# Folded heads loaded ahead of the first attention, and two pairs of them per routing wait, in a two-layer block of attention and feed-forward

## The chip, the cores and the metric

One core of a Trainium2 chip. Times are device microseconds of one launch. The kernel before took 667.93 us, the median of three runs (667.68 to 668.8).

## What is computed

800 tokens (8 batches of 100) of width 512 pass four residual steps, each on a layer norm of the stream: a causal cross attention, a mixture of 8 experts of which each token takes 2, a latent cross attention with 16 heads, and a feed-forward with quantised weights and activations. Cut to what the change touches:

```python
x = x + _L0_xattn_ref(_layernorm(x), ctx_512, Wq, Wkv_expand, Wout)
x = x + _L0_ffn_ref(_layernorm(x), Wg, W1, W2, W3)
x = x + _L1_xattn_ref(_layernorm(x), ctx_512, Wq, w_kc_q, w_kc_kv, W_qr, W_kr, Wo)
x = x + _L1_ffn_ref(_layernorm(x), w_gate_up, w_down)

# in _L0_ffn_ref: each token's two best experts
scores = jnp.einsum('btd,ed->bte', x, Wg)
topk_s, topk_i = jax.lax.top_k(scores, TOP_K)

# in _L1_xattn_ref: three products in a row make the scored query
q_hk = (hidden_q @ Wq.T).reshape(b, s, H, K)
q_big = jnp.einsum('bshk,hkq->bshq', q_hk, w_kc_q)
q_r = jnp.einsum('bshq,hqr->bhsr', q_big, W_qr)
```

The three matrices of the last lines don't depend on the tokens. The kernel multiplies them into one matrix of 512 x 64 per head (the folded heads), in 8 pairs of heads.

## The kernel before

**Tiling.** Tokens lie in seven tiles of 128 rows, the last of 32. All matmuls of the steps that matter here are f32. TensorE (PE), VectorE (DVE) and ScalarE (ACT) run in the order in which the code is written (`tc.manual_schedule`, leaving at the spill branch and entered again behind it). GpSimd (POOL) and the SP queue, which issues most transfers, are ordered by the framework, by priority and by when a buffer comes free; each then works through its queue in that order.

**Stages.** First attention (to about 105 us), with the output projection of the last tiles mixed in; routing; a branch for tokens that no expert has room for; eight experts; second attention; quantised feed-forward. The change lies in the second to fourth, and in what is loaded ahead of the first.

**Folding a pair.** `fold_load(i)` (L698) loads one pair's three matrices in five transfers, some 1.1 MB, into `wq_p`, `kq_p` and `qr_p` of the pool `fw` (three buffers each, opened at L493 when the first attention's inputs are done with). `fold_first` (L722) is twelve recorded matmuls of 64 columns (L711) and a copy by ACT (`a_p`, L719); `fold_second` (L746) four matmuls of 512 columns (L749) and a copy by ACT (`f_p`, L753); `fold_third` four transposes (L759) and a copy by ACT into `wqf` (L760). `fold_beside` and `fold_turn` are another form of the first step for use between an expert's matmuls (L731, L741).

**Routing** (L765 to L835). The tokens of tiles 0 to 4 are scored and ranked first (`gate_scores`, `rank_choices`, `give_slots`), then tiles 5 and 6, whose projection was put last. Each ranking is a row of small DVE steps, with PE needed for the counts (L658, L661) and ACT for one exponential (L631). Then POOL scatters each tile's rows to the slots of their experts (`x_slot`, L686, 13 scatters). There are two stretches in which PE waits for DVE: in each, one pair is folded. Pairs 0 to 2 are loaded during the last batches of the first attention; each further load waits for a buffer.

**Branch.** `spilt` says whether a token found no slot. SP and the engines read it and jump over the block if not, which is so with these inputs. Tiles of the pool `sp` belong to that block.

**After the branch.** SP fetches the slots of experts 0 and 1 (`xg`, L1015), then three row blocks of the quantised feed-forward's weights (`gu`, L850), one of the down projection (`dn`, L855) and one pair. PE folds pairs 2 and 3 meanwhile, then transposes expert 0's slots (`columns_of`, L1040, copied into `xgT` by ACT and DVE, L1044 and L1042), and the experts begin.

**Experts** (L1101 on). Per expert: `gate_and_up` three times (L1109), the down product (L1175), and the next expert's transposes. Between them experts 0 to 3 fold pairs 4 to 7, one each, and load the next. DVE also quantises two blocks of `gu` per expert and, for experts 0 to 3, one of `dn`. Weights of expert e+2 are loaded into `ew` while e runs. Behind the last experts, `wq_p` and `qr_p` serve for output weights of the second attention (`load_wo`, `value_weights`). The rows come back from `x_acc`, and the rotary tables and contexts are loaded into pools that take the place of `ew` and `fw`.

Of the kernel before, what the change touches and what calls it, by code (L numbers as in the profile page):

```python
# [12 lines left out]
F32 = mybir.dt.float32  # L13
# [6 lines left out]
P = 128  # L20
B, S, D = 8, 100, 512
N = B * S
L, DC = 361, 128
KC = D // P
# [15 lines left out]
NH1, R1, CQ = 16, 64, 384  # L40
# [10 lines left out]
def tile_kernel(  # L51
# [7 lines left out]
    nc = tc.nc  # L59

    def open_pool(name, bufs=1, side="left"):
        guard = tc.tile_pool(name=name, bufs=bufs, side=side)
        pool = guard.__enter__()
        return pool, lambda: guard.__exit__(None, None, None)
# [90 lines left out]


    fold, close_fold = open_pool("fold", side="right")
    ate, close_ate = open_pool("attn0_early", side="right")
    at, close_at = open_pool("attn0")
    atw, close_atw = open_pool("attn0w", bufs=2)  # L160
# [28 lines left out]
    for t in range(4, NT):  # L189
# [7 lines left out]
        x_acc[NR:, :].rearrange("(n p) d -> p n d", p=P),  # L197
        zeros.unsqueeze(1).to_broadcast([P, SPARE // P, D]),
    )

    mask = at.tile([S, 4, S], BF16, tag="mask", name="mask")
    nc.gpsimd.memset(mask, 0.0)
# [277 lines left out]
    ew, close_ew = open_pool("ew", bufs=2, side="right")  # L480
# [9 lines left out]

    fw, close_fw = open_pool("fold_in", bufs=3, side="right")  # L493
    wqf = fold.tile([P, KC, NH1 * R1], F32, tag="wqf", name="wqf")

    gp, close_gp = open_pool("gate", side="right")
# [198 lines left out]

    def fold_load(i):  # L698
        wq_p = fw.tile([P, 2, D], F32, tag="wq_p", name=f"wq_p{i}")
        nc.sync.dma_start(wq_p, wq1[ds(2 * i * P, 2 * P), :].rearrange("(j p) d -> p j d", p=P))  # L700
        kq_p = fw.tile([P, 2, CQ // P, P], F32, tag="kq_p", name=f"kq_p{i}")
        qr_p = fw.tile([P, 2, CQ // P, R1], F32, tag="qr_p", name=f"qr_p{i}")
        for j in range(2):
            nc.sync.dma_start(kq_p[:, j], wkcq[2 * i + j].rearrange("(c p) k -> p c k", p=P))
            nc.sync.dma_start(qr_p[:, j], wqr[2 * i + j].rearrange("(c p) r -> p c r", p=P))
        return i, wq_p, kq_p, qr_p

    def fold_head(i, wq_p, kq_p, qr_p, j, pa=None):
        pa = bank() if pa is None else pa
        for c in range(CQ // P):  # L710
# [11 lines left out]
    def fold_first(*loads):  # L722
        pa = fold_head(*loads, 0)
        return fold_copy(*loads, fold_head(*loads, 1, pa))
# [21 lines left out]
    def fold_second(i, wq_p, a_p):  # L746
        pb = bank()
        for j in range(2):
            nc.tensor.matmul(  # L749
                pb[ds(R1 * j, R1), :], a_p[:, ts(j, R1)], wq_p[:, j, :], start=True, stop=True  # L750
            )
        f_p = fw.tile([P, D], F32, tag="f_p", name=f"f_p{i}", bufs=2)
        nc.scalar.copy(f_p, pb)  # L753
        return i, f_p

    def fold_third(i, f_p):
        pt = bank()
        for c in range(KC):
            nc.tensor.transpose(pt[:, ts(c, P)], f_p[:, ts(c, P)], ident)  # L759
        nc.scalar.copy(wqf[:, :, ts(i, P)], pt.rearrange("p (c r) -> p c r", c=KC))  # L760

    pairs_left = list(range(3, NH1 // 2))
    loaded = [fold_load(i) for i in range(3)]


    begin(6)
    po = bank()
    project_part(2, po, oT, wout_sb, KC, 0, 2)
# [34 lines left out]
    project_part(5, po, oT, wout_sb, KC, 0, KC)  # L803
    rank_choices(0, 5)
    give_slots(0, 5)
    part = fold_first(*loaded.pop(0))
    project_add(5, po)
    token_stats(mvs, 5, 6)
    token_scales(mvs, sd_all, rstd_all, 5, 7)
    nc.scalar.activation(sd0[:, 0:1], ln_eps, AF.Exp)  # L810
    for t in range(5, 7):
        gate_norm(t)
    part = fold_second(*part)
    loaded.append(fold_load(pairs_left.pop(0)))
    xT = gate_columns(5, 7)
    fold_third(*part)
    gate_scores(5, 7, xT)

    part = fold_first(*loaded.pop(0))
    rank_choices(5, 7)  # L820
    give_slots(5, 7)

# [6 lines left out]
    nc.vector.tensor_reduce(most, pn[:, :NE], AX.X, ALU.max)  # L829
    spilt = gp.tile([P, 1], I32, tag="spilt", name="spilt")  # L830
    nc.vector.tensor_scalar(spilt, most, float(CAP), None, ALU.is_gt)
    part = fold_second(*part)
    fold_third(*part)
    close_atw()
    close_at()  # L835

# [9 lines left out]
    def load_gate_up(n, pool=None):  # L846
        w = rows.tile([P, D], F32, tag="xn", name=f"gu{n}") if pool else qin.tile(
            [P, D], F32, tag="gu", name=f"gu{n}", bufs=GB
        )
        nc.sync.dma_start(w, wgu[ts(n, P), :])  # L850
        return n, w

    def load_down(n):
        w = qin.tile([P, NI], F32, tag="dn", name=f"dn{n}", bufs=1)
        nc.sync.dma_start(w, wdn[ts(n, P), :])  # L855
        return n, w
# [27 lines left out]
    gate_up_left = list(range(OT - LATER))  # L884
    HC = len(SLOTS)
    GB = 3
    gate_up_in = []

    def quantise_next():
        if gate_up_in:  # L890
            turn_gate_up(*quantise_gate_up(*gate_up_in.pop(0)))
            if gate_up_left:
                gate_up_in.append(load_gate_up(gate_up_left.pop(0)))

    in_order.__exit__(None, None, None)

    def slot_tiles(e):
# [15 lines left out]
    with tc.If(spills > 0, preferred_fallthrough_block=True):  # L913
# [38 lines left out]
        with tc.For_i(0, NE, 1, hint_engines=()):  # L952
            nc.gpsimd.iota(at_x, pattern=[[0, 1]], base=0, channel_multiplier=1)
            w12_e = sp.tile([P, KC, 2 * HE], F32, tag="spw", name="spw")
            for c in range(KC):
                gathered(w12_e[:, c, :], w12.rearrange("e d h -> (e d) h"), at_w[:, c : c + 1])
            w3_e = sp.tile([P, 3, D], F32, tag="sp3", name="sp3")
            for m, (m0, mr) in enumerate(HCH):
                gathered(
                    w3_e[:mr, m, :], w3.rearrange("e h d -> (e h) d"),  # L960
                    at_w[:mr, KC + m : KC + m + 1],
                )
            nc.vector.tensor_scalar(at_w[:, :KC], at_w[:, :KC], D, None, ALU.add)
            nc.vector.tensor_scalar(at_w[:, KC:], at_w[:, KC:], HE, None, ALU.add)
            with tc.For_i(0, NT, 1, hint_engines=()):
                x_t = sp.tile([P, D], F32, tag="spx", name="spx")
                gathered(x_t, x_all_rows, at_x)
                g_t = sp.tile([P, 1], F32, tag="spg", name="spg")
                gathered(g_t, spilt_gates, at_g)
                pt = bank()  # L970
                for c in range(KC):
                    nc.tensor.transpose(pt[:, ts(c, P)], x_t[:, ts(c, P)], ident)
                xT = sp.tile([P, KC, P], F32, tag="spxT", name="spxT")
                nc.scalar.copy(xT, pt.rearrange("p (c q) -> p c q", c=KC))
                hT = sp.tile([P, 3, P], F32, tag="sph", name="sph")
                for m, (m0, mr) in enumerate(HCH):
                    pw = bank()
                    ups = [(0, UP[m], mr)] if m < 2 else [(0, UP64, 64), (64, HE, 32)]
                    for j, cols in enumerate(([(0, m0, mr)], ups)):
                        for to, at_col, n in cols:  # L980
                            for c in range(KC):
                                nc.tensor.matmul(
                                    pw[ds(to, n), ds(j * P, P)], w12_e[:, c, ds(at_col, n)],
                                    xT[:, c, :], start=(c == 0), stop=(c == KC - 1),
                                )
                    s = sp.tile([P, P], F32, tag="sps", name="sps")
                    nc.scalar.activation(s[:mr], pw[:mr, :P], AF.Silu)
                    nc.vector.tensor_tensor(hT[:mr, m, :], s[:mr], pw[:mr, ds(P, P)], ALU.mult)
                py = bank()
                for m, (m0, mr) in enumerate(HCH):  # L990
                    nc.tensor.matmul(
                        py[:, :D], hT[:mr, m, :], w3_e[:mr, m, :], start=(m == 0), stop=(m == 2)
                    )
                y_t = sp.tile([P, D], F32, tag="spy", name="spy")
                nc.vector.tensor_scalar(y_t, py[:, :D], g_t, None, ALU.mult)
                nc.gpsimd.indirect_dma_start(
                    out=x_acc, out_offset=bass.IndirectOffsetOnAxis(ap=at_x, axis=0),
                    in_=y_t, in_offset=None, compute_op=ALU.add,
                )
                nc.vector.tensor_scalar(at_x, at_x, P, None, ALU.add)  # L1000
                nc.vector.tensor_scalar(at_g, at_g, P, None, ALU.add)
# [75 lines left out]

    behind_slots = tc.issue_after(slots[1][-1][1])
    behind_slots.__enter__()
    gate_up_in = [load_gate_up(gate_up_left.pop(0)) for _ in range(GB)]  # L1080
    down_in = load_down(0)
    while len(loaded) < 3:
        loaded.append(fold_load(pairs_left.pop(0)))


# [4 lines left out]
    in_order.__enter__()  # L1090

    nc.scalar.activation(most, ln_eps, AF.Silu)
    part = fold_first(*loaded.pop(0))
    following = fold_first(*loaded.pop(0))
    part = fold_second(*part)
    following = fold_second(*following)
    fold_third(*part)
    fold_third(*following)
    turned = columns_of(0, slots[0])
    gates = choices(0, slots[0])  # L1100

    for e in range(NE):
# [35 lines left out]
        part = None  # L1138
        gate_and_up(0)
        if loaded:  # L1140
            part = fold_beside(*loaded.pop(0))
            if pairs_left:
                loaded.append(fold_load(pairs_left.pop(0)))
        quantise_next()
        gate_and_up(1)
        if part:
# [77 lines left out]
    value_weights(6)  # L1224
    normed.append(layernorm(1))
    value_weights(7)
    close_fw()
    close_ew()

# [606 lines left out]
```

## Time and profile before

| what | us |
| --- | --- |
| median of three runs | 667.93 |
| the profiled execution's own time | 667.63 |
| its span, first to last instruction | 665.9 |
| PE matmul busy | 637.0 (96%) |
| DVE busy | 416.8 (63%) |
| ACT busy | 243.5 (37%) |
| POOL busy | 177.7 (27%) |
| mean granted PE clock | 0.979 |

The page cuts the span into 40 slices of 16.6 us; a digit is the busy share in tenths, PEclk the granted clock in tenths of full speed. A table by stage gives, for each stretch, its length and the busy time (and number) of instructions of each engine, then granted clock, share of the DMA engines, and GB/s. A line of the timeline has the start, the time, engine, line, operation, what is written from what, and in brackets how long the engine had been idle and what ended it. A matmul's end is modelled, its start is recorded. The chain of waits follows the work that ended last backwards; here it can be followed to 134 us and not further back, so the routing is read from the timeline.

### The profile page before, as it was taken

What the parts mean: (1) busy time and instruction counts of PE and PEld (TensorE: products, weight loads), DVE (VectorE), ACT (ScalarE), POOL (GpSimd) and SP (SyncE); (2) the same over time, 40 slices, a digit from 0 to 9 for tenths busy, and PEclk for the clock granted to TensorE, in tenths of its full rate; (3) what the DMA queues carried; (4) which work ended last, traced back from release to release, by engine and by line L of the source; (5) the groups of instructions that cost most, each with busy time, mean ns of one, the idle gap of its engine ahead of it and who ended that gap; (6) DMA issues with size and microseconds to landing.
All of it is one profiled execution on the core that took longest, in us unless ns stands there. A gap on an engine that the chain in (4) does not pass through costs nothing.

```text
span 665.9 us, 9840 instructions
## 1 busy us (share of the span) xinstructions
PE 637.0 (96%) x3471; PEld 411.5 (62%) x3471; DVE 416.8 (63%) x1058; ACT 243.5 (37%) x558; POOL 177.7 (27%) x191
## 2 busy tenths in 40 slices
PE   8999998689999999999999999999999999999995
PEld 5767755366677677558866766766666544444443
DVE  4865688407666553253148877877676456666687
ACT  3653454332212111231145655655555313222140
POOL 2232330600111122228604233234233002221021
PEclk9999999569999999999999999999999999999998
DMA  9800293789999998754300210210000301011211
GB/s 302 250 18 17 67 331 122 242 258 287 313 303 307 267 338 213 157 163 122 110 1 11 65 45 17 59 36 11 1 13 0 118 13 29 10 31 30 50 31 70
DMA packets 80289, 80.34 MB, mean 121 GB/s; under 512 B 41267, under 2 KB 54119, under 8 KB 80111
## 3 DMA queue, kind: packets, MB, share of 16 engines
q1 hardware_dynamic: 76543, 70.97, 36.4%
q0 software_dynamic: 3696, 8.72, 5.8%
q8 instruction: 28, 0.46, 0.3%
q14 instruction: 22, 0.18, 0.1%
HBM read 56.36 MB, written 16.50 MB: 109 GB/s over the span
## 4 chain that ended last, share of the span: by engine, by line
PE 66%; DVE 5%; DMA 4%; POOL 1%; ACT 1%; issue 1%; SPq 1%; POOLq 0%; ACTq 0%; DVEq 0%
PE bank L359 12%; PE bank L1109 11%; PE bank L1407 10%; PE bank L1382 8%; PE bank L1325 7%; PE bank L1175 6%; PE bank L1399 4%; PE bank L1566 3%; PE bank L1363 2%; PE bank L1040 1%; DMA qr_p<-in_wqr 1%; POOL e L1393 1%; DVE nm L1386 1%; DMA x_acc<-y,place 1%; DMA gu<-in_wgu 1%
## 5 line engine op out<-in xcount | busy, mean ns | idle before, releaser
L1393 POOL TENSOR_SCALAR e<-e,rs 128x361 f32<-128x361 f32 x51 | 61.4, 1205 | 126.2 <-DVE rs L1392 84.6
L359 PE MATMUL bank<-wvo,ctxT 128*128 128x512 f32 x192 | 83.9, 593 | 0.0
L1382 PE MATMUL bank<-kvT,qe 128*128 128x361 f32 (+1 forms) x208 | 78.6, 475 | 1.7 <-issue 1.0
L1109 PE MATMUL bank<-xgT,w 128*128 128x240 f32 (+1 forms) x384 | 75.5, 369 | 0.9 <-ACT xgT L1044 0.9
L1407 PE MATMUL bank<-pT,kvr 121*128 121x400 f32 x192 | 70.6, 503 | 1.4 <-ACT pT L82 0.8
L1109 PEld LDWEIGHTS bank<-xgT,w 128*128 128x128 f32 (+1 forms) x384 | 64.1, 181 | 12.4 <-issue 6.6
L1390 ACT ACTIVATE e<-bank,nm 128x361 f32<-128x361 f32 x100 | 56.5, 565 | 30.9 <-DVE nm L1386 21.9
L1386 DVE TENSOR_REDUCE nm<-bank 128x1 f32<-128x361 f32 x100 | 52.7, 528 | 17.3 <-PE bank L1382 16.6
L1399 PEld LDWEIGHTS bank<-ident,e 128*121 128x121 f32 x300 | 46.6, 184 | 26.9 <-POOL e L1393 3.9
L359 PEld LDWEIGHTS bank<-wvo,ctxT 128*128 128x128 f32 x192 | 36.2, 190 | 43.1 <-issue 42.6
L1186 POOL DMA_INDIRECT x_acc<-y,place x16 | 24.5, 1531 | 122.1 <-ACT y L1185 118.8
L1583 POOL TENSOR_TENSOR hid<-g,u 128x512 f32<-128x512 f32 (+1 forms) x17 | 20.5, 1215 | 114.2 <-ACT g L1574 74.8
L1399 PE MATMUL bank<-ident,e 128*121 128x128 f32 x300 | 49.6, 275 | 1.0 <-POOL e L1393 1.0
L1407 PEld LDWEIGHTS bank<-pT,kvr 121*128 121x128 f32 x192 | 33.9, 190 | 20.9 <-ACT pT L82 1.0
L1325 PE MATMUL bank<-xT,wqf 128*128 128x256 f32 (+1 forms) x192 | 43.8, 389 | 0.7 <-ACT xT L1310 0.7
L1175 PE MATMUL bank<-w,hT 128*128 128x512 f32 (+3 forms) x96 | 43.0, 595 | 0.3 <-DVE hT L1133 0.3
L324 POOL TENSOR_TENSOR s<-s,rs 100x800 f32<-100x800 f32 x16 | 24.4, 1523 | 70.7 <-DVE rs L323 30.5
L1325 PEld LDWEIGHTS bank<-xT,wqf 128*128 128x128 f32 x192 | 36.2, 190 | 7.4 <-ACT xT L1310 0.9
L1382 PEld LDWEIGHTS bank<-kvT,qe 128*128 128x128 f32 (+1 forms) x208 | 32.0, 186 | 11.7 <-issue 1.8
L82 ACT COPY pT<-bank 121x384 f32<-121x384 f32 (+3 forms) x55 | 24.4, 443 | 25.5 <-PE bank L1399 24.8
L80 DVE COPY ctxT<-bank 128x400 f32<-128x400 f32 (+2 forms) x23 | 13.2, 572 | 31.8 <-PE bank L1325 26.0
L1121 DVE TENSOR_TENSOR hT<-silu,bank 128x240 f32<-128x240 f32 x16 | 6.5, 404 | 38.0 <-ACT silu L1120 38.0
(260 smaller groups left out, 1022.2 us busy)
## 6 DMA issues: line engine op xcount, KB each, us to landing
w<-in_w SPq DMA_DIRECT2D x8, 1408.0 KB
gu<-in_wgu SPq DMA_DIRECT2D x22, 256.0 KB
w<-in_w SPq DMA_DIRECT2D x16, 256.0 KB
wq_p<-in_wq SPq DMA_DIRECT2D x8, 512.0 KB
wo<-in_wo SPq DMA_DIRECT2D x8, 512.0 KB
x_slot<-zeros SPq DMA_DIRECT2D x1, 3840.0 KB
kq_p<-in_wkcq SPq DMA_DIRECT2D x16, 192.0 KB
dn<-in_wdn SPq DMA_DIRECT2D x4, 704.0 KB
```

Of the source, the lines that this page charges most:

```text
L82: nc.scalar.copy(dst, src)
L359: nc.tensor.matmul(po[:, :D], lhs[:, c, ds(t * P, r)], rhs[:, c, :], start=(c == 0), stop=(c == chunks - 1),)
L1109: nc.tensor.matmul(po, w12_e[:, c, cols], xgT[:, c, :], start=(c == c0), stop=(c == c1 - 1))
L1175: nc.tensor.matmul(py[i][:n], hT[:mr, m, ds(s0, n)], w3_e[:mr, m, :], start=(m == 0), stop=(m == 2))
L1186: d = nc.gpsimd.indirect_dma_start(out=x_acc, out_offset=bass.IndirectOffsetOnAxis(ap=place[:, 0:1], axis=0), in_=y, in_offset=None, compu ...
L1325: nc.tensor.matmul(pq[:, i, :], wqf[:, c, ts(p0 + i, P)], xT[:, c, :], start=(c == 0), stop=(c == KC - 1),)
L1382: nc.tensor.matmul(ps[ds(to, n), :L], qe[:, ds(k0, n)], kvT, start=True, stop=True)
L1386: d = nc.vector.tensor_reduce(nm[:r], ps[:r, :L], AX.X, ALU.max, negate=True)
L1390: nc.scalar.activation(e[:r], ps[:r, :L], AF.Exp, bias=nm[:r], accum_out=sm[:r])
L1393: (nc.vector if odd else nc.gpsimd).tensor_scalar_mul(e[:r], e[:r], rs[:r])
L1399: nc.tensor.transpose(pt[:LP, c, :r], e[:r, ds(c * (LP - 1), LP)], ident[:r, :r])
L1407: nc.tensor.matmul(pc[:, :VC], kvr[:, c, :], pT[:, c, :], start=(c == 0), stop=(c == LC - 1))
```

## The change

1. The pool `fw` is opened ahead of the first attention's pools, with four buffers instead of three, and `fold_load` with it. Pairs 0 to 3 are loaded behind the first attention's inputs. Since `fw` now lies under the first attention's pool, the routing's tiles (`gp`) take part of the place of that pool.
2. In both routing waits two pairs are folded instead of one. After the first, two pairs are loaded instead of one.
3. The first three `gu` blocks and the first `dn` block are loaded ahead of the branch instead of behind the slot fetches. The pairs still left are then all loaded behind the slot fetches, and none in the experts.
4. So six pairs are folded ahead of the experts, and two beside experts 0 and 1.
5. The spill block uses the row tiles `xs` in place of five tiles of its own, and `ew` is closed before `fw`.

```diff
     fold, close_fold = open_pool("fold", side="right")
+    fw, close_fw = open_pool("fold_in", bufs=4, side="right")
     ate, close_ate = open_pool("attn0_early", side="right")
...
+    def fold_load(i):
...
+    pairs_left = list(range(4, NH1 // 2))
+    loaded = [fold_load(i) for i in range(4)]
...
-    fw, close_fw = open_pool("fold_in", bufs=3, side="right")
...
-    pairs_left = list(range(3, NH1 // 2))
-    loaded = [fold_load(i) for i in range(3)]
...
     give_slots(0, 5)
-    part = fold_first(*loaded.pop(0))
+    parts = [fold_first(*loaded.pop(0)) for _ in range(2)]
     project_add(5, po)
     token_stats(mvs, 5, 6)
     token_scales(mvs, sd_all, rstd_all, 5, 7)
     nc.scalar.activation(sd0[:, 0:1], ln_eps, AF.Exp)
     for t in range(5, 7):
         gate_norm(t)
-    part = fold_second(*part)
-    loaded.append(fold_load(pairs_left.pop(0)))
+    parts = [fold_second(*a) for a in parts]
+    for _ in range(2):
+        loaded.append(fold_load(pairs_left.pop(0)))
     xT = gate_columns(5, 7)
-    fold_third(*part)
+    for a in parts:
+        fold_third(*a)
     gate_scores(5, 7, xT)
 
-    part = fold_first(*loaded.pop(0))
+    parts = [fold_first(*loaded.pop(0)) for _ in range(2)]
     rank_choices(5, 7)
     give_slots(5, 7)
...
-    part = fold_second(*part)
-    fold_third(*part)
+    parts = [fold_second(*a) for a in parts]
+    for a in parts:
+        fold_third(*a)
     close_atw()
     close_at()
...
-    gate_up_in = []
...
+    gate_up_in = [load_gate_up(gate_up_left.pop(0)) for _ in range(GB)]
+    down_in = load_down(0)
     in_order.__exit__(None, None, None)
...
-                x_t = sp.tile([P, D], F32, tag="spx", name="spx")
+                x_t = xs[1]
...
     behind_slots = tc.issue_after(slots[1][-1][1])
     behind_slots.__enter__()
-    gate_up_in = [load_gate_up(gate_up_left.pop(0)) for _ in range(GB)]
-    down_in = load_down(0)
-    while len(loaded) < 3:
+    while pairs_left:
         loaded.append(fold_load(pairs_left.pop(0)))
...
         gate_and_up(0)
         if loaded:
             part = fold_beside(*loaded.pop(0))
-            if pairs_left:
-                loaded.append(fold_load(pairs_left.pop(0)))
...
     value_weights(7)
+    close_ew()
     close_fw()
-    close_ew()
```

More of the change, by code (lines that the diff above doesn't have):

```diff
@@ L199, in tile_kernel @@
     )
+    def fold_load(i):
+        wq_p = fw.tile([P, 2, D], F32, tag="wq_p", name=f"wq_p{i}")
+        nc.sync.dma_start(wq_p, wq1[ds(2 * i * P, 2 * P), :].rearrange("(j p) d -> p j d", p=P))
+        kq_p = fw.tile([P, 2, CQ // P, P], F32, tag="kq_p", name=f"kq_p{i}")
+        qr_p = fw.tile([P, 2, CQ // P, R1], F32, tag="qr_p", name=f"qr_p{i}")
+        for j in range(2):
+            nc.sync.dma_start(kq_p[:, j], wkcq[2 * i + j].rearrange("(c p) k -> p c k", p=P))
+            nc.sync.dma_start(qr_p[:, j], wqr[2 * i + j].rearrange("(c p) r -> p c r", p=P))
+        return i, wq_p, kq_p, qr_p
+    pairs_left = list(range(4, NH1 // 2))
+    loaded = [fold_load(i) for i in range(4)]
     mask = at.tile([S, 4, S], BF16, tag="mask", name="mask")
@@ L694, in give_slots @@
                 tc.add_to_no_dep_group("to_slots", d.ins)
[L698 to L706, printed above, removed]
     def fold_head(i, wq_p, kq_p, qr_p, j, pa=None):
@@ L972, in tile_kernel @@
                     nc.tensor.transpose(pt[:, ts(c, P)], x_t[:, ts(c, P)], ident)
-                xT = sp.tile([P, KC, P], F32, tag="spxT", name="spxT")
+                xT = xs[2].rearrange("p (c q) -> p c q", c=KC)
                 nc.scalar.copy(xT, pt.rearrange("p (c q) -> p c q", c=KC))
-                hT = sp.tile([P, 3, P], F32, tag="sph", name="sph")
+                hT = xs[3][:, : 3 * P].rearrange("p (m q) -> p m q", m=3)
                 for m, (m0, mr) in enumerate(HCH):
@@ L985, in tile_kernel @@
                                 )
-                    s = sp.tile([P, P], F32, tag="sps", name="sps")
+                    s = xs[4][:, :P]
                     nc.scalar.activation(s[:mr], pw[:mr, :P], AF.Silu)
@@ L993, in tile_kernel @@
                     )
-                y_t = sp.tile([P, D], F32, tag="spy", name="spy")
+                y_t = xs[5]
                 nc.vector.tensor_scalar(y_t, py[:, :D], g_t, None, ALU.mult)
@@ L1092, in tile_kernel @@
     nc.scalar.activation(most, ln_eps, AF.Silu)
[L1093 to L1098, printed above, removed]
+    parts = [fold_first(*loaded.pop(0)) for _ in range(2)]
+    parts = [fold_second(*a) for a in parts]
+    for a in parts:
+        fold_third(*a)
     turned = columns_of(0, slots[0])
```

## The prediction

> **What bounds the kernel now.** I read the slices first, then busy time by stage, then the timeline around the two routing waits, and last the chain of waits. The slices:
>
> ```profile
> span 665.9 us, 9840 instructions
> ...
> PE   8999998689999999999999999999999999999995
> ...
> PEclk9999999569999999999999999999999999999998
> DMA  9800293789999998754300210210000301011211
> ```
>
> TensorE is the bound nearly everywhere, except in slices 7 and 8 (116 to 150 us), where it has gaps and its clock is halved: the routing. By stage (span; busy us of PE, PEld, DVE, ACT, POOL; granted clock; DMA share; GB/s):
>
> ```profile
> 115.20:118.90 3.70, 1.12 (x5) 0.24 (x5) 3.10 (x12) 2.70 (x4) 2.56 (x3) 1.00 0.64 174
> 118.90:123.00 4.10, 3.57 (x24) 2.35 (x24) 0.64 (x2) 2.47 (x6) 3.19 (x4) 0.59 1.05 313
> 123.00:128.60 5.60, 3.37 (x23) 3.04 (x21) 2.63 (x18) 0.00 (x0) 4.27 (x5) 0.50 0.85 327
> 128.60:134.40 5.80, 3.09 (x8) 1.01 (x9) 3.06 (x18) 2.59 (x5) 2.26 (x3) 0.50 0.24 96
> 134.40:139.70 5.30, 5.27 (x24) 5.19 (x24) 0.00 (x0) 0.71 (x3) 0.58 (x1) 0.50 0.44 109
> ...
> 183.00:200.60 17.60, 17.60 (x91) 12.34 (x89) 11.84 (x29) 3.97 (x10) 3.06 (x2) 1.00 1.13 309
> ...
> 233.50:248.70 15.20, 15.20 (x70) 11.00 (x69) 8.14 (x24) 2.38 (x5) 3.05 (x2) 1.00 1.08 334
> ```
>
> An expert with a folded pair beside it takes 17.6 us, one without 15.2, PE full in both: a pair costs 2.4 us there. In the routing PE has 2 to 3 us free in each wait. The timeline there:
>
> ```profile
> 113.65 1.52 PE L711 MATMUL bank<-qr_p,kq_p 128*128 128x64 f32 x12
> ...
> 115.49 1.28 ACT L240 ACT_TABLE_LOAD   x1
> ...
> 118.86 1.09 PE L578 MATMUL bank<-ident,x_all 128*128 128x128 f32 x8 [2.26 <-DVE x_all L560]
> ...
> 128.62 0.27 ACT L719 COPY a_p<-bank 128x128 f32<-128x128 f32 x1 [6.39 <-remote]
> ...
> 144.63 0.98 PE L1040 MATMUL bank<-ident,xg 128*128 128x128 f32 x8
> ```
>
> The same L711 block takes 1.52 us at full clock and 2.82 (from 123.02) at half. The copy at 128.62 comes 2.78 us after the modelled end of its multiplications (125.84) and no row says why. L1040, which starts the experts, waits for the half-clock fold work in front of it (134.43 to 144.5). The chain of waits:
>
> ```profile
> 134.08 3.58 DMA x_slot<-x_all,to
> ...
> 144.41 6.66 DMA qr_p<-in_wqr
> 151.12 0.87 PE bank L731 x10
> ```
>
> The last scatter lands at 137.66, the slots are then fetched, and expert 0 stalls once more for a pair loaded late.
>
> **The change by parts.** Of eight pairs, four are folded ahead of the experts now (one per wait, two after the branch), four beside experts 0 to 3. After: six ahead (two, two, two) and two beside experts 0 and 1.
>
> *Experts 2 and 3.* Each loses 2.4 us of PE work. DVE becomes near-critical: after its product at 191.45 it runs without a break to the copy of xgT (L1042) at 199.71; PE from the end of the second gate_and_up (190.58) needs 2.59 + 0.97 + 5.15 = 8.71 without the fold, to 199.3. PE so waits 0.45 us for DVE: 1.95 each, **3.9** in sum (bounds 0, if the transfers bound this stage, and 4.8). Transfers: two pairs of 1.1 MB fewer there, and experts 4 to 6 run at 15.2 with shares of 0.9 to 1.2.
>
> *Expert 0.* It takes 18.85 us against 17.61 of expert 1. Its pair will be queued behind four slot fetches alone, not behind gu, dn and another pair as well: five issues of 0.45 us after 140, landed by about 145, needed at 147.5. **1.2** (bound 0).
>
> *First wait.* fold_first twice ends at 113.65 + 3.04 = 116.7, its second a_p copy at 117.0. The sqrt table load, which stands behind that copy on ACT, moves from 115.49 to 117.0, the sqrt ends at 118.6 instead of 118.03: x_all and the transposes come 0.57 late. PE has 0.86 us of fold_second more, so its gap shrinks from 2.26 to 0.9. ACT then has two f_p copies instead of one ahead of gT (0.47 more) and two wqf copies ahead of parts: parts end at 122.7 instead of 122.2, **0.5 late**. PE's second fold_third (0.55) lies inside that.
>
> *Clock.* It fell at 119.67 and rose at 143.57 by the trace's clock records. In the 3.4 us before the fall PE streamed for 13% (column counts over clock), and every stretch with 28% or more kept the clock. After, the same stretch holds eight L749 matmuls and is at 50%, the next at some 40%: I take full clock.
>
> *Second wait.* At full clock L601 takes half, L711 starts at 123.2, and 24 of it take 3.04: to 126.25, 0.4 after 125.84. Queued behind them on PE: the slot counts (L658, L661); on ACT the exponential that DVE waits for. The unexplained 2.78 us is bounded by 0 (the blocks at 113.65 and 134.43 had none) and 2.78 (same place, same instruction). I keep it whole, as that row is the nearest. So counts, scatter and branch come **0.4 late**.
>
> *Transfers in the routing.* More than before: one pair (1.1 MB) and gu and dn moved ahead of the branch (3 x 256 + 704 KB), 2.6 MB, 8 us at 320 GB/s. Room, by the shares above, from 115.2 to 134.4: 0.36 x 3.7 + 0.15 x 5.6 + 0.76 x 5.8 = 6.6 us. Up to 1.4 us runs over into the last scatter's landing; I take half, **0.7**.
>
> *After the branch.* PE starts at 134.85; 24 of L711 3.04, eight of L749 1.72, the rest 1.3: done at 141, where it took 10.1 us to 144.5. The second slot tile landed at 141.6 by the semaphore records; now 141.6 + 0.4 + 0.7 = 142.7, which becomes what L1040 waits for. 144.52 - 142.7 = **1.8** earlier.
>
> *Costed at nothing.* Four pairs ahead of attention: 4.4 MB, some 15 us, behind all its inputs on SP's queue, in 27 to 50 us where the DMA share is 0.03 to 0.08 and SP idles until 46; twenty issues of 0.47 us. Were that cover gone, x_acc rows would be late, which nobody reads before the first expert adds. POOL's 27 memsets and iotas for the routing (2.2 us at 2.5 to 4.8) now lie in memory that xn0 frees only during attention: POOL ends a share at 80.11 that PE takes at 81.94, so 1.8 is covered, 0.4 at most not. The second pair of loads in the first wait is five more issues on SP (2.3 us from 118); behind them are the x_acc rows of tiles 5 and 6, which no wait in the routing reads. The gu and dn loads, four issues of 0.4 us moved past the slot fetches, wait in SP's queue until L601 frees their place (123); behind them is the read of the spill flag at 132.85, so nine microseconds cover them, and a longer wait would delay the branch by its excess. The gate weights' load goes behind the four pairs and is wanted at 106. At the end the rotary tables can wait for the last value_weights (292.6) instead of 287.99; POOL would finish at 332 instead of 329 and PE takes the first rows at 339.8. Code in the spill branch isn't run.
>
> **Sum.** 1.8 + 1.2 + 3.9 = 6.9 us from the profiled execution's 667.63 (665.9 of span and 1.7 around it): 660.7. The median shown is 667.93, 0.3 more: **661.0**.
>
> **Rivals.**
> *No pause.* The 2.78 us aren't there again: scatter 2.4 early, the second slot tile at 139.9, PE ready at 138.5: 4.6 instead of 1.8, **658.2**. For it: two of three L711 blocks without pause; against: the same place.
> *The clock falls all the same*, at about 122, since PE then does little but transposes with waits between. L711 runs 124.9 to 130.2, the scatter is 1.6 late, and PE, at half clock with two pairs more ahead of the branch, reaches L1040 at 147.4: 2.9 late, less 5.1 of the experts: **665.7**. Against: a stretch at 28% kept the clock at 99 us. [...]
> *The slow block (slower).* If 123.02 to 128.6 was a rate, 465 ns per L711 multiplication under the transfers of that moment, and not a pause, and the clock is at half, 24 of them take 11.2 us from 124.9: the counts come at 136.1, 7.5 late, PE has fold work until 143.5, the branch's block runs 10.7 more, L1040 starts at 154.2, 9.7 late. Less 5.1: **672.5**. It decides as soon as L1040 comes after 149.6. For it: traffic in that wait grows; against: L711 at 134.43 went at 223 ns.
> *It does nothing*: transfers bound the experts (share 1.1), so that less PE work there is idle time, and the routing is 1 us slower for the ACT copies: **667.5**. Against: experts 4 to 6.
>
> **Numbers.** Forecast 0.43, no pause 0.24, clock falls 0.20, slow block 0.10, nothing 0.03. The first three are faster by over 0.2% (1.3 us, what a measurement of this kernel can tell): 0.87; same 0.03; slower 0.10. The range leaves the slow block out and takes in the others: from 656.5 (no pause, and experts 2 and 3 at nearly 2.4 each) to 666.5.
>
> **What would show it.** Experts 2 and 3 at 15.2 to 15.7 us; expert 0 without a wait for qr_p; clock 1.00 from 115 to 135 (or 0.5: the third case); the time from the end of L711 to the a_p copy in the second wait; L1040 waiting for xg and not for L759. The forecast is wrong if L1040 starts after 144.5 or if the experts don't shorten.

## The result and the profile after

| | us |
| --- | --- |
| before, median of six runs | 667.8 (667.22 to 670.63) |
| after, median of six runs | 663.75 (662.83 to 664.68) |
| ratio after / before | 0.991, 95% interval 0.9883 to 0.9938 |
| the profiled execution after: time, span | 663.5, 661.3 |
| mean granted PE clock | 0.988 |

The change makes the kernel 4.05 us faster; 6.9 were forecast. The edit moves the lines: L711, L749 and L759 of before are L714, L752 and L762 after, L593 and L597 are L606 and L610, L658 is L671, L719 is L722, L731 is L734, L1040 is L1043, L1109 is L1108. The slices of the page after:

```profile
span 661.3 us, 9868 instructions
...
PE   8999999799999999999989999999999999999995
...
PEclk9999999789999999999999999999999999999999
DMA  9980161989999977564200211110000301011211
```

PE's gap in slices 7 and 8 is down to one slice, but the clock still falls there. By stage (first the routing, then one expert with a pair beside it, one from which the pair was taken, one that never had one; columns as before: span; busy us of PE, PEld, DVE, ACT, POOL; granted clock; DMA share; GB/s):

```profile
115.20:119.57 4.37, 3.40 (x23) 1.91 (x22) 3.34 (x13) 3.02 (x5) 2.44 (x3) 1.00 0.61 176
119.57:124.78 5.21, 3.27 (x29) 2.39 (x29) 0.58 (x2) 3.29 (x8) 3.99 (x5) 0.89 0.99 308
124.78:131.28 6.50, 5.60 (x35) 5.51 (x34) 2.64 (x18) 0.32 (x2) 3.46 (x4) 0.50 1.08 379
131.28:137.45 6.17, 5.58 (x17) 2.27 (x17) 2.96 (x18) 2.53 (x6) 2.85 (x3) 0.51 0.95 378
137.45:143.41 5.96, 5.81 (x40) 4.12 (x41) 0.00 (x0) 3.75 (x8) 0.00 (x0) 1.00 0.65 185
163.70:181.31 17.61, 17.61 (x91) 12.35 (x90) 11.85 (x29) 3.97 (x10) 3.15 (x2) 1.00 1.10 315
181.31:197.13 15.82, 15.37 (x69) 10.84 (x68) 11.21 (x25) 2.41 (x6) 3.37 (x3) 1.00 1.14 304
213.03:228.31 15.28, 15.28 (x68) 11.09 (x69) 8.67 (x29) 2.35 (x5) 2.74 (x2) 1.00 1.04 281
```

The third and fourth rows are the second routing wait: half clock, and transfers at 380 GB/s where before they went at 327 and 96. In the row from 181.31 PE is busy for 15.37 of 15.82 us. The missing 0.45 us lie ahead of expert 3, where the profile names no releaser, but PE starts right behind DVE's copy of xgT:

```profile
196.41 0.62 DVE L1045 COPY xgT<-bank 128x448 f32<-128x448 f32 x1
...
197.13 0.65 PE L1108 MATMUL bank<-xgT,w 128*128 128x240 f32 x2 [0.45 <-issue]
```

The timeline of the second wait:

```profile
121.75 0.48 PE L606 MATMUL bank<-gT,wg_sb 128*32 128x160 f32 x8
...
123.70 0.29 ACT L610 COPY parts<-bank 128x160 f32<-128x160 f32 x1 [1.12 <-PE bank L606]
...
124.78 5.38 PE L714 MATMUL bank<-qr_p,kq_p 128*128 128x64 f32 x24
...
129.95 0.22 PE L671 MATMUL bank<-both,before 128*128 128x16 bf16 x1
...
130.96 0.43 ACT L722 COPY a_p<-bank 128x128 f32<-128x128 f32 x2 [6.97 <-PE bank L826]
...
133.67 0.98 POOL L699 DMA_INDIRECT x_slot<-x_all,to  x1 [4.51 <-DVE tmp L684]
...
137.45 2.86 PE L714 MATMUL bank<-qr_p,kq_p 128*128 128x64 f32 x24 [0.59 <-PEq L916]
...
143.41 0.98 PE L1043 MATMUL bank<-ident,xg 128*128 128x128 f32 x8
```

The copy of `parts` comes 1.5 us after the modelled end of the scores (L606), the 24 multiplications take 5.38 us, the counts (L671) stand behind them, and the first of the last scatters comes at 133.67, 2.1 us later than before. Yet PE reaches expert 0's transposes 1.2 us earlier, because the clock is back at 137.3 and the block after the branch runs at full speed. These transposes (L1043) follow the fold's (L762) with no wait for the slots. What follows, by the chain of waits:

```profile
143.10 6.22 DMA qr_p<-in_wqr
149.46 0.84 PE bank L734 x10
```

Expert 0 again stalls for the last load of its pair. Taking the first product of each expert as its start, the two profiled executions compare so:

| stretch | forecast gain | before | after | gain |
| --- | --- | --- | --- | --- |
| start of expert 0 | 1.8 | 146.53 | 145.22 | 1.31 |
| expert 0 | 1.2 | 18.86 | 18.48 | 0.38 |
| experts 2 and 3 | 3.9 | 17.61, 17.61 | 15.83, 15.90 | 3.49 |
| experts 1, 4 to 6 | 0 | 63.24 | 63.31 | -0.07 |
| from expert 7 to the end | 0 | 402.1 | 402.6 | -0.5 |
| around the span | 0 | 1.7 | 2.2 | -0.5 |
| sum | 6.9 | | | 4.1 |

The last two rows are hardly the work of the change: from expert 7 on the code differs only in the order in which two pools are closed, and that part took 401.9 to 403.2 us in the fourteen profiled executions of this study, 402.1 and 402.6 in the two of the kernel before.

### The profile page after: what moved, and what is told of

Its sections match the earlier page's. It is cut to its first block, busy times and chain, and to the rows that moved or that the text cites. A ratio compares the mean times of both kernels' runs of the same rounds, so it can differ in the third digit from the quotient of the medians.

```text
span 661.3 us, 9868 instructions
## 1 busy us (share of the span) xinstructions
PE 635.1 (96%) x3469; PEld 411.3 (62%) x3469; DVE 416.1 (63%) x1058; ACT 241.9 (37%) x556; POOL 177.3 (27%) x191
## 4 chain that ended last, share of the span: by engine, by line
PE 64%; DVE 7%; DMA 2%; ACT 2%; POOL 1%; issue 1%; SPq 0%; ACTq 0%; POOLq 0%; DVEq 0%
PE bank L373 12%; PE bank L1108 11%; PE bank L1404 9%; PE bank L1379 7%; PE bank L1322 7%; PE bank L1172 6%; PE bank L1396 4%; PE bank L1563 3%; PE bank L1211 2%; DMA gu<-in_wgu 1%; DVE nm L1383 1%; PE bank L1043 1%; DMA qr_p<-in_wqr 1%; ACT e L1387 1%; POOL e L1390 1%
## 5 line engine op out<-in xcount | busy, mean ns | idle before, releaser
L1108 PE MATMUL bank<-xgT,w 128*128 128x240 f32 (+1 forms) x384 | 74.8, 369 | 1.7 <-issue 0.9
L1108 PEld LDWEIGHTS bank<-xgT,w 128*128 128x128 f32 (+1 forms) x384 | 64.3, 181 | 13.5 <-issue 5.2
L1580 POOL TENSOR_TENSOR hid<-g,u 128x512 f32<-128x512 f32 (+1 forms) x17 | 20.5, 1217 | 114.1 <-ACT g L1571 74.8
L80 DVE COPY pT<-bank 121x384 f32<-121x384 f32 (+3 forms) x57 | 28.7, 503 | 2.3 <-PE bank L1396 2.3
```

The source lines that it names most:

```text
L80: nc.vector.tensor_copy(dst, src)
L1108: nc.tensor.matmul(po, w12_e[:, c, cols], xgT[:, c, :], start=(c == c0), stop=(c == c1 - 1))
```

## The experiments

Three sets, each on a chip of its own (called chip A, B and C); medians are compared within a set.

| set | kernel | median us | ratio to before (95%) |
| --- | --- | --- | --- |
| A | before | 667.29 | |
| A | order | 663.41 | 0.9936 (0.9911 to 0.996) |
| A | hole_pair | 662.89 | 0.9938 (0.9912 to 0.9963) |
| A | hole_matmuls, one run | 663.57 | |
| A | hole_transposes, one run | 662.53 | |
| B | before | 666.19 | |
| B | early_one_each | 664.20 | 0.9966 (0.9945 to 0.9986) |
| B | pairs_12 | 661.12 | 0.9918 (0.9891 to 0.9945) |
| B | hole_12_late | 660.38 | 0.9905 (0.987 to 0.9939) |
| B | hole_12_late_fill | 658.58 | 0.9888 (0.9846 to 0.993) |
| C | before | 669.23 | |
| C | before_again, one run, profiled | 677.37 | |
| C | after_again | 664.41 | 0.9911 (0.9878 to 0.9944) |
| C | late_12 | 664.53 | 0.991 (0.9877 to 0.9943) |
| C | best_again (hole_12_late_fill again) | 665.65 | 0.9936 (0.9913 to 0.9959) |

From the traces, in us (the start of expert 0, how long each of the first four experts took, when PE was at half clock ahead of 150):

| kernel | start | e0 | e1 | e2 | e3 | half clock |
| --- | --- | --- | --- | --- | --- | --- |
| before | 146.53 | 18.86 | 17.61 | 17.61 | 17.61 | 119.7 to 143.6 |
| after | 145.22 | 18.48 | 17.61 | 15.83 | 15.90 | 123.6 to 137.3 |
| order | 145.83 | 17.68 | 17.61 | 15.82 | 21.03 | 125.1 to 132.0, 135.4 to 142.2 |
| hole_pair | 143.58 | 20.00 | 17.61 | 15.82 | 15.90 | 127.8 to 131.2, 134.6 to 138.1, 141.5 to 148.3 |
| hole_matmuls | 145.15 | 18.70 | 17.61 | 15.82 | 15.90 | 133.0 to 143.2 |
| hole_transposes | 143.90 | 19.60 | 17.61 | 15.82 | 15.89 | 131.5 to 141.7 |
| early_one_each | 143.52 | 17.68 | 17.61 | 17.61 | 17.61 | 119.8 to 140.2 |
| pairs_12 | 143.31 | 15.89 | 17.68 | 17.61 | 15.82 | 124.4 to 131.2, 134.6 to 141.4 |
| hole_12_late | 141.97 | 15.89 | 17.68 | 17.61 | 15.82 | 126.4 to 129.8 |
| hole_12_late_fill | 142.07 | 15.89 | 17.68 | 17.61 | 15.86 | none |
| before_again | 146.44 | 19.68 | 17.61 | 17.61 | 24.88 | 119.5 to 143.4 |
| after_again | 144.46 | 18.69 | 17.61 | 15.82 | 15.90 | 124.2 to 134.4 |
| late_12 | 147.85 | 15.90 | 17.68 | 17.61 | 15.82 | 123.9 to 134.1, 137.5 to 144.3 |
| best_again | 148.32 | 15.89 | 17.68 | 17.61 | 15.82 | 124.7 to 138.4 |

A part of the differences in the start lies ahead of the routing's folds: the first fold begins anywhere from 112.88 to 113.88 us in these executions, at 113.65 in before and 113.87 in after. Counted from it, the experts start after 32.88 us in before and 31.35 in after, 33.04 in before_again and 31.52 in after_again: a gain of 1.5 us in both comparisons.

**order: the counts ahead of the second pair.**

```diff
-    parts = [fold_first(*loaded.pop(0)) for _ in range(2)]
+    parts = [fold_first(*loaded.pop(0))]
     rank_choices(5, 7)
     give_slots(5, 7)
     ...
+    parts.append(fold_first(*loaded.pop(0)))
```

> The changed kernel with the second pair of the second routing wait put behind the slot counts on TensorE: 12 L714 multiplications stand ahead of the counts instead of 24. Theory queue (the last scatter is 2.1 us late in the changed kernel because the counts and DVE's exponential stand behind 24 multiplications at half clock): the counts start when DVE is ready, at about 128.2 instead of 129.95, and the scatters come 2 us earlier, at about 131.6, 132.9 and 134.2; the total stays within 0.5 us of the changed kernel (663.2 to 664.0), because TensorE's own work, the same sum at half clock, ends no earlier than 143. Rival late completion (TensorE's completions are seen late in this stretch whatever is queued, 2.8 us late before and 3.3 us late after for the first pair): the counts are seen at 130 to 131 again and the scatters move by less than 0.7 us.

The counts came at 125.44 and the scatters at 128.67 to 131.19, 5 us earlier, more than expected, as in this execution the `parts` copy wasn't late either (121.64, right behind its scores) and the first pair's multiplications ran at full clock. The edit isn't what did this. hole_matmuls and hole_transposes (below, same chip) keep both pairs ahead of the counts and have them at 126.32 and 126.02; pairs_12 on chip B, whose routing is that of the changed kernel, has them at 125.91 and its last scatter at 131.53. So the theory of the queue isn't shown. The total stayed where it was expected, 663.41. Two lines of the trace say why the early scatters bring nothing at once:

```profile
131.19 0.91 POOL L699 DMA_INDIRECT x_slot<-x_all,to  x1 [0.30 <-DVEq L917]
...
139.28 1.75 SPq L1019 DMA_DIRECT2D xg<-x_slot  x4
```

The slots are fetched 8 us after the last scatter's issue (3.0 in the changed kernel, 3.7 before). So their issue no longer sets the fetch. The profiled execution also lost 5 us in expert 3, by the chain of waits:

```profile
200.44 8.23 DMA dn<-in_wdn
208.66 0.02 issue
208.69 1.63 DVE amax L147
```

DVE stands in order behind a row block of the down projection that landed late; PE then waits 3.7 us for hT. It isn't tied to the edit: before_again shows the same stall (12.8 us from issue to landing, expert 3 of 24.88 us).

**hole_pair, hole_matmuls, hole_transposes: the hole ahead of L614.** The hole is the time in which PE idles between the gate scores (L606) and their sum (L614). hole_pair puts a pair's multiplications there:

```diff
+        if between:
+            between()
         pg = bank()
...
-    gate_scores(5, 7, xT)
+    gate_scores(5, 7, xT, lambda: parts.append(fold_first(*loaded.pop(0))))
```

In the other two `between` is two multiplications of zeros, or three times four transposes of zeros.

> The changed kernel with one of the second wait's pairs multiplied (L714 x12, 1.5 us) between the gate scores (L606) and their sum over parts (L614), where TensorE stood idle for 1.8 us. [...] Rival PE isn't the bound there (the slot fetch is): no gain, 663.5.

> The changed kernel with two plain multiplications of zeros (128 x 384, some 1.3 us in sum at full clock) in the hole between the gate scores and their sum over parts. Nothing else is changed; their results are not read. [...]

> The same hole filled with twelve transposes of zeros (some 1.3 us in sum at full clock) instead of plain multiplications; their results are not read. [...]

All three kept the clock past 123.6, where the changed kernel lost it, to 127.8, 133.0 and 131.5; order, on the same chip with nothing in the hole, lost it at 125.1 (one execution each). Transposes served as well as multiplications. In hole_pair the scatters again ended at 131.20 and the fetch came only at 138.37; the experts started 1.6 us earlier than in the changed kernel (0.8 of it there at the first fold), and then:

```profile
143.58 5.80 PE L1111 MATMUL bank<-xgT,w 128*128 128x240 f32 x16 [0.82 <-issue]
149.31 0.88 PE L736 MATMUL bank<-kq_p,qr_p 128*64 128x128 f32 x12
```

Sixteen products took 5.80 us at half clock instead of 3.48, and the pair was reached at 149.31. In all four kernels of this set PE gets on with that pair at 149.2 to 149.6, whether the experts start at 143.6 or 145.8, but not for one reason. In hole_matmuls and hole_transposes it waits 0.62 and 1.52 us for the last `qr_p`; hole_transposes starts 1.25 us ahead of hole_matmuls and ends expert 0 only 0.35 ahead. In order (149.23, expert 0 at 17.68) and hole_pair no wait for the load shows: in the first the experts start late, in the second the half clock takes 2.3 us. hole_pair's distance to order in total is inside the intervals: no gain is shown.

**pairs_12: the last two pairs beside experts 1 and 2.**

```diff
-        if loaded:
+        if e and loaded:
             part = fold_beside(*loaded.pop(0))
```

> The changed kernel with the last two pairs beside experts 1 and 2 instead of 0 and 1; nothing else. Theory (every gain ahead of 149 us is swallowed: in the changed kernel and in the four kernels tried so far TensorE comes to L734, expert 0's pair, at 149.3 to 149.6, although the experts start anywhere from 143.6 to 145.8, because that pair's last load lands only then): expert 0 takes about 15.5 us and ends 0.5 to 0.9 us earlier, pairs 6 and 7 are there long before experts 1 and 2; total 662.7 to 663.2 against 663.5. Rival (another transfer, gu, dn or expert 1's weights, is late just behind it, since the queues are full there): no gain.

Expert 0 takes 15.89 us, expert 1 17.68 and expert 2 17.61: no wait for a pair is left. Experts 0 to 3 take 67.0 us in sum against 67.8 in the changed kernel. The median, 661.12, can't be set against 663.5 of another chip; the 0.8 is read from the traces.

**early_one_each: the early loads without the second pairs.** `range(2)` becomes `range(1)` at both waits and at the loads of the first.

> The changed kernel's early loads (four pairs ahead of the first attention, gu and dn ahead of the branch) with the old share of the pairs: one in each routing wait, two behind the branch, four beside experts 0 to 3. Theory (the early loads cost nothing; the whole gain beside experts 2 and 3 comes from folding two pairs more in the routing): experts 2 and 3 take 17.6 us each again, pair 4 is there before expert 0 so that its wait goes, routing about 0.5 to 1 us shorter: 665.5 to 667. Rival (the experts were quicker because the loads were out of their way): experts 2 and 3 take 16 us or less and the total is 664.

The wait of expert 0 is gone (17.68), experts 2 and 3 take 17.61 each: the theory holds for both. The median is 664.20, below the expected 665.5, against 666.19 for before on this chip, a gain of 2.0. Expert 0 accounts for 1.2 of it, which leaves 0.8 for the routing; before has no trace on this chip. pairs_12 on the same chip is 3.1 faster than this: what the two pairs more in the routing are worth, once nothing waits for the others.

**hole_12_late and hole_12_late_fill: transfers, then the clock.** The first is hole_pair and pairs_12 together, and:

```diff
-    gate_up_in = [load_gate_up(gate_up_left.pop(0)) for _ in range(GB)]
-    down_in = load_down(0)
     in_order.__exit__(None, None, None)
     ...
     behind_slots.__enter__()
+    gate_up_in = [load_gate_up(gate_up_left.pop(0)) for _ in range(GB)]
+    down_in = load_down(0)
```

The second adds 6, 8 and 6 transposes of the identity.

> Three things at once on the changed kernel: a pair multiplied in the hole between the gate scores and their sum, the last pairs beside experts 1 and 2, and the gu and dn loads (1.5 MB) back behind the slot fetches. Theory (the scatters' own transfers stand behind the loads: with the scatters issued 5 us earlier the slot fetch still came at 138.4, 7.2 us after the last scatter's issue, against 3.6 before, while the transfers ran at 390 GB/s): 1.5 MB less in front are 3 to 4 us; the fetch comes at 134.5 to 135.5, the experts' first products at 140.5 to 142 and, as no pair is waited for in expert 0, the total is 659.5 to 661. Rival 1 (TensorE's own work before the experts is the bound): fetch early, but experts not before 142.5; 661.5. Rival 2 (gu and dn, now late, stall DVE in expert 0): the gain is given back inside expert 0, 662.5 to 663.5.

> The kernel hole_12_late with twenty transposes of the identity that nobody reads (6 after the second wait's last pair, 8 ahead of the branch, 6 ahead of the experts), where TensorE would idle. [...] Rival (the transfers are the bound there, the clock costs nothing): the same time as hole_12_late within 0.4 us.

Last scatter and fetch of pairs_12, then of hole_12_late, same chip:

```profile
131.53 0.91 POOL L699 DMA_INDIRECT x_slot<-x_all,to  x1 [0.30 <-DMA gu<-in_wgu]
...
138.14 1.75 SPq L1018 DMA_DIRECT2D xg<-x_slot  x4
```

```profile
131.64 0.91 POOL L701 DMA_INDIRECT x_slot<-x_all,to  x1 [0.30 <-issue]
...
136.08 2.05 SPq L1020 DMA_DIRECT2D xg<-x_slot  x4
```

The same moment of issue, and a fetch 2.1 us earlier with 1.5 MB less in front of it. The filled hole doesn't explain this: hole_pair has it too, with the loads in front, and fetches 7.2 us after its last scatter's issue, against 4.4 here. From 134.6 to 138.1 us the DMA share is 0.31 here and 0.61 in pairs_12; from 133 to 136 it is 1.05 in hole_pair. So the loads in front do hold the scatters' landing up. The forecast of 3 to 4 us was too much. Experts start at 141.97 and the total is 660.38, inside the first theory's range; expert 0 shows no stall for the late gu and dn. The twenty transposes of the second kernel removed the last half-clock stretch, but the experts start at the same time (142.07): where the clock had fallen, PE then waited for the slots anyway. Its median is 1.8 us lower with the same trace up to expert 7 within 0.2 us, and its rest took 401.9 against 403.2; so that the fill itself gains is not shown.

**The last set.**

> The kernel before, unchanged, profiled once more on another chip. Theory (the 2.78 us between the end of the second wait's multiplications and the a_p copy, which the prediction kept whole as a property of the place, came with that one execution: the same place with the same twelve multiplications had no such time in early_one_each): the copy comes within 0.5 us of the modelled end, and the experts start up to 2.5 us earlier than 146.5. Rival (it belongs to the kernel before): the copy is 2 to 3 us late again.

> The changed kernel, unchanged, once more, on the chip of the kernels it is compared with. [...] Rival (the late completions at 121.9 and 127.6 belong to the changed kernel): they are there again, with the fall at 123.6 or within 0.5 us of it.

> The kernel pairs_12 with one thing changed: the gu and dn loads (1.5 MB) back behind the slot fetches. Theory transfers (the last scatter is issued at 131.5 in pairs_12 and its slots are fetched at 138.1, because the loads stand in front of it): the fetch comes 2 us earlier, at about 136, as it did in hole_12_late (136.1). TensorE's half-clock work ahead of the experts (to 141.5 in pairs_12) is then the bound, so the total falls by less than the fetch does: 660.4 to 661.2 against 661.1. Rival (the hole, not the loads, moved the fetch in hole_12_late): it stays at 138.

> The kernel hole_12_late_fill once more, beside the changed kernel on the same chip. If the three causes found (late load of expert 0's pair, transfers ahead of the scatters, clock) are what kept the change below its forecast, it is 4 to 5.5 us faster than the changed kernel here: 658 to 659.5.

before_again falsified its theory: the a_p copy came at 128.53, 2.9 us after the modelled end, as in the first execution. after_again had its late completions too (the copy of `parts` 1.6 us late, the first pair seen 4.1 us late) and the clock's fall at 124.2, 0.6 us later than in the first execution; its total is 664.41, and its pair was reached at 148.92, 0.5 us sooner than there. late_12 adds nothing on transfers: on this chip its last scatter was issued at 135.51, 4 us later than in pairs_12, so fetch (138.51) and total don't answer the question. best_again was expected 4 to 5.5 us faster than the changed kernel and is 1.2 slower. Its trace:

```profile
127.86 0.27 ACT L724 COPY a_p<-bank 128x128 f32<-128x128 f32 x1 [4.76 <-issue]
129.95 0.17 DVE L620 COPY score<-bank 128x8 f32<-128x8 f32 x1 [10.05 <-remote]
...
130.13 0.27 ACT L724 COPY a_p<-bank 128x128 f32<-128x128 f32 x1 [2.00 <-remote]
```

The scores' sum (L616) was issued at 123.16 and should have ended at 123.7; DVE took it up at 129.95. PE had its whole queue issued by 126.7 and then waited for DVE. In hole_12_late_fill, the same kernel in set B, the counts came at 126.94; here at 132.77. The experts start 6.2 us later, and the rest is alike to 0.1 us.

So the late completions don't belong to a place in the code, nor to the kernel before. They show in the first executions of before and after and in all four of set C, and in none of the eight of sets A and B, each on one chip. What holds PE's completions back is open; all that the runs show is where (120 to 131 us) and how much. The transfers alone don't explain it: from 120.4 to 130.6 us they run at 360 GB/s in hole_12_late_fill, which has no late completion, and at 359 in after, which has.

## Why the forecast was right, and where it wasn't

The change is faster, as forecast, but by 4.05 us and not by 6.9. The total of 663.75 is nearer to the 665.7 of the rival "the clock falls all the same" than to the 661.0 of the forecast.

**Experts 2 and 3: right.** 1.95 each was forecast from 2.4 us less PE work and a 0.45 us wait for DVE. A gap of 0.45 us behind DVE's copy is there; 1.78 and 1.71 were gained. The bound of 0 (transfers limit this stage) is out, at a DMA share of 1.14.

**Expert 0: the step that failed.** "Landed by about 145, needed at 147.5" counted five issues of 0.45 us after 140 and no time in the queues. The last of the five was issued at 143.10 and took 6.22 us to land, at 149.32, in a stretch with a DMA share of 1.08, behind the slots and the pair's other loads. The row to cost it by stood in the chain of waits before: the same load, 6.66 us from issue to landing. Of 1.2 us 0.4 were gained. early_one_each (17.68) shows that the full 1.18 is there for a pair that is loaded in time. This miss also hides others: in hole_transposes most of an earlier start ends in this wait.

**Start of the experts: the sum near by luck, its parts wrong.** 1.31 instead of 1.8. What was to become the bound, the second slot tile, isn't one: L1043 waits for no slot, it follows PE's own fold work. The first wait's delay was right up to the transposes: they start 0.71 us later, of which 0.22 were there at 78 us already, and 0.57 had been forecast. "I take full clock" was wrong: it fell at 123.6. The reading behind it, that every stretch with 28% or more kept the clock, went by column counts; by the time that TensorE was busy the 3.41 us ahead of the fall, from 120.2, are at 0.56 (1.91 us), against 0.34 (1.15 us) ahead of the fall in before. The fall itself is the rival "the clock falls all the same", at the place it named; its price was wrong, because the rival kept half clock until the experts, whereas the clock rose at 137.3 and the block after the branch took 5.96 us (6.1 in the forecast, at full clock).

**The pause kept whole: it came again, elsewhere.** It is there for the first pair (3.36 us, from the modelled end at 127.60 to the copy at 130.96) but lies beside the second pair's multiplications, so that the counts came late by the half clock and by the 1.5 us ahead of `parts`. pairs_12, with the same routing on chip B, is without it: its last scatter is issued at 131.53 and not at 136.22, and its experts start 1.05 us sooner after the first fold. "No pause" was the better rival there, not here.

**Transfers in the routing: 0.7, hidden here.** The scatters were late themselves, so their landing wasn't: fetch 3.0 us after the last issue, against 3.7 before. Where they come early, the loads cost 2.1 us for gu and dn alone. "Costed at nothing" for moving them was thus right only under cover of the late scatters.

**Early loads at no cost: right as far as seen.** early_one_each is faster than before, not slower, and the first fold of the routing begins at 112.9 to 113.9 in the twelve executions with the early loads, at 113.4 and 113.65 in the two without. **The slow block** didn't come: 24 multiplications took 5.38 us, 224 ns each, not 465. **Does nothing** is out.

**What is left** of the miss of 2.8 us: expert 0 0.8, start 0.5, experts 2 and 3 0.4, and 1.0 in rows that the change hardly touches.

No version here is shown to beat the changed kernel on every chip. On chip B hole_12_late_fill is at 0.9888 of before; on chip C the same kernel loses to the changed one. pairs_12 keeps the routing as it is and only moves a wait; it wasn't run on chip C.

## What to carry to other kernels

Cost a load that is issued into full queues from issue to landing by a row with the same DMA share (6.66 us before, 6.22 after), not by the number of issues; the first wait behind the place that an edit speeds up is looked up before its gain is counted. A time between an engine's modelled end and the next start that no row explains is measured on a second chip before it enters a sum. And judge an edit by the length of each stage in several traces, since one median can hold a stall of 5 us that it didn't make.

## What the runs showed of the hardware

**When the clock fell, and for how long.** The half-clock stretches ahead of 150 us (table of the traces above) are 3.4, 6.8, 10.2, 13.7, 20.5 and 23.9 us long, and they begin anywhere from 119.5 to 141.5. The one of before lasts 23.89 us (119.67 to 143.56), the one of after 13.65 (123.61 to 137.26). In a stretch as long as the shortest of these, 3.41 us, ahead of the fall TensorE was busy, by modelled times, for 1.15 us in before (0.34), 1.91 in after (0.56) and 2.82 in pairs_12 (0.83), the last 1.9 of these with the fold's 64-column multiplications. A fall came after a busy stretch too, so that the busy share alone doesn't tell when; what does is not shown.

**Transposes with the clock kept.** In pairs_12 the 3.42 us ahead of these, from 117.53, were followed by full clock:

```profile
117.53:120.95 3.42, 2.32 (x22) 1.63 (x24) 1.45 (x4) 3.39 (x7) 2.58 (x3) 1.00 0.92 227
```

```profile
118.71 0.99 PE L591 MATMUL bank<-ident,x_all 128*128 128x128 f32 x8 [0.97 <-DVE x_all L573]
...
119.83 1.14 PE L762 MATMUL bank<-ident,f_p 128*128 128x128 f32 x8
```

2.32 of 3.42 us busy (0.68), and all but 0.2 of it are these transposes. hole_pair has the same two blocks from 118.77 to 121.02 and kept the clock to 127.8. With the hole filled by twelve transposes (1.53 us) the clock was kept to 131.5, by multiplications of zeros (1.56 us) to 133.0, one execution each: no difference of kind between the two is shown.

**Completions of TensorE seen up to 6 us late** on chip C (2.9 us in before_again, 6.2 in best_again) and in the first executions (2.8 in before, 3.4 in after), and in none of the eight on chips A and B, are the largest difference between chips here, and the reason why hole_12_late_fill is the fastest on one and slower than the changed kernel on the other.
